# Two mixer layers and a mixture of experts: other DRAM layouts for the reloads, rows fetched earlier from one token tensor, a gate computed in a later stage

## The chip, the cores and the metric

The kernel runs on one core of a Trainium2 chip. Time is the device time of one execution in microseconds (us), the median of several runs. The core has five engines: PE (matrix products; weight loads are listed as PEld), DVE (vector), ACT (activation functions and copies), POOL (general, also issues the indirect transfers) and SP (issues most of the plain transfers). They run in parallel, each in its own program order, and wait for each other by semaphores. Transfers between DRAM and on-chip memory run on 16 DMA engines.

## The reference, cut to what matters

The input is four images of 256 channels and 64 x 64 positions, so 16384 tokens. Everything is float32.

```python
# layer 0: a selective-scan mixer of 512 channels and 16 states, gated by z
tokens = x.transpose(0, 2, 3, 1).reshape(Bb, Hh * Ww, Cc) @ w_in.T
z = sigmoid(silu(tokens @ w_gate.T + b_gate))
t = layernorm(tokens) * ln_g + ln_b
xm, zm = split(t @ in_w.T)
xm = silu(causal_conv4(xm))                    # four taps
dt = softplus(dbl[..., :16] @ dt_w.T + dt_b)   # dbl = xm @ xproj_w.T; B and C are its rest
h = exp(dt * A) * h + (dt * xm) * B            # along the tokens, per channel and state
y = (sum_over_states(h * C) + D * xm) * silu(zm)
x = x + tokens + (y @ out_w.T) * z @ w_out.T
# layer 1: a second mixer with 8 heads and 64 states, then a mixture of 8 experts
t = t + mixer1(layernorm(t))
e = argmax(softmax(layernorm(t) @ gate_w + gate_b))     # one expert per token, with a capacity
t = t + nan_to_num(prob * (relu(layernorm(t) @ w1[e] + b1[e]) @ w2[e] + b2[e]))
```

## The kernel before, in words

The kernel has three phases one after the other: `mixers` (both mixers and the routing), `experts` and `turn` (the result is transposed back into the image layout).

In `mixers` the tokens are cut into 64 chunks of T = 256 tokens, channels on the 128 partitions. A chunk passes through `front0` (input product, layer norm, the first convolution), `mid0` (dt and u), `scan`, `tail0`, `front1`, `ssd` and `back1`. The order of instructions on each engine is not the order of the code: all operations are noted in a `Plan`, each with a time slot (`k_.at(n)`, 16 slots to a chunk, n relative to the chunk's first scan step), an estimated duration and its dependencies, and a list scheduler (`Plan.order`) puts them in an order in which several chunks overlap. This is why nearly all instructions of the mixers carry line 373. FRONT0, MID0, TAIL, SSD and BACK are the first slots of the stages; loads are noted AHEAD = 4 slots early. A tile has a tag and a number of buffers; a new tile of a tag waits until an old one is free.

Data that must move to other partitions goes through DRAM. The convolution wants four taps of 32 channels on 128 partitions: `to_taps` (685) stores `raw`, and `tapped` (691) loads `raw4`, four channel groups with four DMAs, one for each tap. The scan works on tiles of 32 channels x 4 states on the partitions and 4 channel groups x 256 tokens along them: `mid0` stores dt, u and the B and C rows, and `scan` (832) loads `dt4`, `u4` and `bc4`, four DMAs each, and `gx` (silu(zm) and xm). One scan step `u` of 16 is: ACT makes four decays `da`, DVE multiplies `ub` and runs the scan `h`, POOL multiplies `p` by C, PE sums over the states into `py`. There are two buffers each of dt4, u4, gx and h, three of da and p. In `ssd` the decays of layer 1 are summed, stored as `sums_d` and loaded as `cdec`, once for each half chunk.

In all these DRAM tensors the 256 tokens of one channel are contiguous, so that a partition is filled in runs of 1 KB.

The gate `z` of layer 0 is multiplied in `front0` (733) into the first two rows of `pre0`, goes through silu and, by `half_tanh`, to tanh, is stored as `z_d` and reloaded in `tail0`, where x is loaded once more (`xtail`). `silus` (649) gathers the silu calls, since they need a table load on ACT before and behind them; no other table function may stand between.

`back1` stores a chunk's tokens twice, as `tok_d` (the tokens) and `out_d` (where the experts' results go), and POOL scatters for each token a small record `meta` (probability, scale, shift, token number) into the slots of its expert.

`experts` runs over 72 blocks, 63 of 256 slots and 9 of 128, in the order of `line_up`. This phase is ordered by the tile framework's own scheduler. `ahead` (1378) gathers a block's `meta`, casts the token number to an integer (`number`, four buffers) and gathers the expert's weights `w`, 2.2 MB; `begin` (1390) gathers the tokens `rows` from `tok_d`, normalizes them on ACT (`tn`), and has PE transpose them (`pt`, `xt`). Then PE makes the eight hidden products `ph` (ReLU on ACT and DVE: `hid`), and the output product `po`; DVE and ACT make `y` and `fixed`, adding `rows`, and POOL scatters the result to `out_d`. Gathers and scatters are indirect DMAs on POOL's queue, two per block of 256.

`turn` loads 1024 tokens at a time from `out_d`, transposes them on PE and stores the image.

Of the kernel before, what the change touches and what calls it, by code (L numbers as in the profile page):

```python
# [43 lines left out]
TAIL, SSD, BACK = 18, 29, 37  # L44
# [332 lines left out]
def tile_conv_attn_hybrid(ctx: ExitStack, tc: tile.TileContext, a: dict, out: bass.AP, cap: int, st: int):  # L377
# [6 lines left out]
    NB, _, L = x.shape  # L384
    NCH = L // T
# [13 lines left out]
    out_d = dram1.tile([NT, C], F32, name="out_d")  # L399
# [25 lines left out]
    def mixers(es):  # L425
# [215 lines left out]
        def load_x(k_, tag):  # L641
            xin = work([P, KC, T], tag)
            r.dma("SP", xin, x[k_.b].rearrange("(k p) l -> p k l", p=P)[:, :, k_.c * T : (k_.c + 1) * T])
            return xin
# [4 lines left out]
        def silus(*tiles, gates=0):  # L649

            def weight(t):
                return 0.06 + Plan.width(t) / 1130

            load = 1.3
            calls = [(weight(t), nc.scalar.activation, (t, t, AF.Silu), t, t) for t in tiles]
            calls += [(weight(t[:, :KC]), half_tanh, (t[:, :KC],), t[:, :KC], t[:, :KC]) for t in tiles[:gates]]
            calls[0] = (calls[0][0] + load, *calls[0][1:])
            calls.append((load, nc.scalar.preload_act_table_set, (SETS,), None, None))
            r.acts(calls)
# [21 lines left out]
        def spread_rows(d):  # L681

            return d.rearrange("(j g) c l -> (g c) j l", g=SQ)

        def to_taps(raw, tag):

            d = scratch([raw.shape[1] * SQ, R, TAPS - 1 + T], tag)
            r.dma("SP", spread_rows(d), raw)
            return d

        def tapped(d, j):
            t = work([P, SQ, T], "raw4", 3)
            for k in range(TAPS):
                r.dma(
                    "SP",
                    t[k * R : (k + 1) * R],
                    d[j * SQ : (j + 1) * SQ, :, k : k + T].rearrange("g c l -> c g l"),
                )
            return t

        def convolve_taps(raw4, weights, j, dst, bias, get):
            pi = get(T)
            for i in range(SQ):
                r.mm(pi[i * R : (i + 1) * R], weights[:, j * SQ + i], raw4[:, i], start=True, stop=True)
# [15 lines left out]
        def front0(k_):  # L720
# [11 lines left out]
            k_.pre0 = pre0 = work([P, KC + 2 * KD, T], "pre0")  # L732
            pg = bank_a(KC, T)
            for m in range(KC):
                for k in range(KC):
                    r.mm(pg[:, m], w_gate[:, k, m * P : (m + 1) * P], xin[:, k], start=k == 0, stop=k == KC - 1)
            for m in range(KC):
                r.act(pre0[:, m], pg[:, m], AF.Identity, bias=b_gate[:, m : m + 1])
# [10 lines left out]
            for half in range(2):  # L749
                k_.at(FRONT0 + 3 + half)  # L750
                for mp in range(2):
# [6 lines left out]
                    for m in range(2):  # L758
                        j = mp * 2 + m
                        o = half * KD + j  # L760
                        dst = raw[:, j, TAPS - 1 :] if half == 0 else pre0[:, KC + j]
# [4 lines left out]
            for j in range(KD):  # L766
# [3 lines left out]
                convolve_taps(part, taps_m, j, pre0[:, KC + KD + j], m_cb, bank_a)  # L770

        def mid0(k_):

            pre0 = k_.pre0
            xs = pre0[:, KC + KD :]

            k_.at(MID0)
            k_.gx_d = scratch([2 * KD, P, T], "gx_d")
            r.dma("SP", k_.gx_d.rearrange("k p l -> p k l"), pre0[:, KC:])
            k_.z_d = scratch([KC, P, T], "z_d")  # L780
            r.dma("SP", k_.z_d.rearrange("k p l -> p k l"), pre0[:, :KC])
# [3 lines left out]
            for k in range(KD):  # L785
                r.mm(pd[:rows], m_xp[:, k], xs[:, k], start=k == 0, stop=k == KD - 1)
# [3 lines left out]
            r.dma("SP", k_.bc_d.rearrange("p s q l -> (p s q) l"), dbl[DTK:])  # L790
            e = work([P, KD, T], "mid", 2)
            dt = work([P, KD, T], "mid", 2)
            for mp in range(2):
# [18 lines left out]
                r.gps("tensor_tensor", e[:, two], dt[:, two], xs[:, two], ALU.mult)  # L812
            k_.at(MID0 + 6)
            k_.dt_d = scratch([NG, R, T], "dt_d")
            r.dma("SP", spread_rows(k_.dt_d), dt)
            k_.at(MID0 + 7)
            k_.u_d = scratch([NG, R, T], "u_d")
            r.dma("SP", spread_rows(k_.u_d), e)
# [13 lines left out]
        def scan(k_):  # L832
# [3 lines left out]
            for fp in range(2):  # L836
                k_.at(fp * 4 - AHEAD)
                t = work([P, SQ, T], "bc4", 3)
                for q in range(SQ):
                    src = k_.bc_d[fp, :, q]  # L840
# [3 lines left out]
            for jp in range(2):  # L844
                loaded = []
                for jj in range(2):
                    j = jp * 2 + jj
                    both = []
                    for name, src in (("dt4", k_.dt_d), ("u4", k_.u_d)):
                        k_.at(jp * 8 + jj * 2 - AHEAD)  # L850
                        t = work([P, SQ, T], name, 2)
                        for q in range(SQ):
                            r.dma(
                                "SP", t[q * R : (q + 1) * R], src[j * SQ : (j + 1) * SQ].rearrange("g c l -> c g l")
                            )
# [3 lines left out]
                gx = work([P, 2, 2, T], "gx", 2)  # L859
                for s in range(2):  # L860
                    r.dma("SP", gx[:, s], k_.gx_d[s * KD + jp * 2 : s * KD + jp * 2 + 2].rearrange("j p l -> p j l"))
# [11 lines left out]
                for i in range(8):  # L873
# [25 lines left out]
                    if i == 0:  # L899
                        py = bank_y(2, T)  # L900
                        for n in range(2):
                            r.act(py[:, n], gx[:, 1, n], AF.Copy, scale=m_d[:, jp * 2 + n : jp * 2 + n + 1])
# [10 lines left out]
                r.tt(k_.g[:, jp * 2 : jp * 2 + 2], gx[:, 0], py, ALU.mult)  # L913

        def tail0(k_):

            k_.at(TAIL - AHEAD)
            xin = load_x(k_, "xtail")
            z = work([P, KC, T], "z")
            r.dma("SP", z, k_.z_d.rearrange("k p l -> p k l"))  # L920
# [117 lines left out]
        def ssd(k_):  # L1038
# [21 lines left out]
            r.dma("SP", sums_d, sums[:NH])  # L1060
# [8 lines left out]
            for s in range(NS):  # L1069
# [15 lines left out]
                cdec = work([P, hh, Q], "cdec")  # L1085
                for g, hs in enumerate(halves):
                    r.dma("SP", cdec[hs], sums_d[g::2, sl].partition_broadcast(N2))
# [7 lines left out]
                r.gps("tensor_tensor", cdec, cdec, cc[:, None, sl].to_broadcast([P, hh, Q]), ALU.mult)  # L1095
# [22 lines left out]
                for h in range(NH):  # L1118
                    hs, q = halves[h % 2], h // 2
                    r.mm(half(h), state[hs, q], cdec[hs, q], start=False, stop=h == NH - 1, skip_group_check=True)  # L1120
# [14 lines left out]
        def back1(k_):  # L1135
# [23 lines left out]
            for dst in (tok_d, out_d):  # L1159
                r.dma("SP", dst[i0 * P : i0 * P + T].rearrange("(s p) d -> p s d", p=P), row[:, :, :C])  # L1160
# [99 lines left out]
        for i in range(len(chunks) + lag):  # L1260
# [4 lines left out]
            todo = []  # L1265
            if one:
                one.at(MID0)
                todo.append(one.pre0)
            if two:
                two.at(SSD - 1)  # L1270
                todo.append(two.pre1)
            if one:
                one.at(MID0)
                silus(one.pre0, gates=1)
            if two:
                two.at(SSD - 1)
                silus(two.pre1)
            if one:
                for stage in (mid0, scan, tail0, front1):
                    stage(one)  # L1280
# [76 lines left out]
    def experts(es):  # L1357
# [20 lines left out]
        def ahead(nj, i):  # L1378

            w = wp.tile([P, W1 + W2 + KF + C], F32, name=nm("w"), tag="w")  # L1380
            row_at, w_at = tables[nj == 1]
            meta = wk.tile([P, 2, META], F32, name=nm("meta"), tag="meta", bufs=4)[:, :nj]
            for j in range(nj):
                gather(meta[:, j], meta_d, row_at[:, i, j : j + 1], NSLOT + P)
            number = wk.tile([P, 2], U32, name=nm("number"), tag="number", bufs=4)[:, :nj]
            nc.vector.tensor_copy(number, meta[:, :, 3])  # L1386
            gather(w, a["w_exp"], w_at[:, i : i + 1], NE * P)
            return nj, w, meta, number

        def begin(nj, w, meta, number):  # L1390

            st = nj * P
            rows = wk.tile([P, 2, C], F32, name=nm("rows"), tag="rows", bufs=4)[:, :nj]
            for j in range(nj):
                gather(rows[:, j], tok_d, number[:, j : j + 1], NT)
            tn = wk.tile([P, 2, C], F32, name=nm("tn"), tag="tn")
# [15 lines left out]
        now = begin(*ahead(*line_up[0][1:]))  # L1412
        soon = ahead(*line_up[1][1:])
        for at, (_, nj, _) in enumerate(line_up):
# [7 lines left out]
            for f in range(KF):  # L1422
                if f == KF // 2 and at + 1 < len(line_up):

                    now = begin(*soon)
                    soon = ahead(*line_up[at + 2][1:]) if at + 2 < len(line_up) else None
# [158 lines left out]
```

## Time and profile before

| | |
|---|---|
| runs | 6423.47, 6443.36, 6457.77 us, median 6443.36 |
| profiled execution | 6421.74 us, its span 6420.0 us |
| mean granted TensorE clock | 0.935 |
| mixers | first token store at 273.0, last at 5181.3 us |
| experts | first gather of rows at 5206.0, last scatter at 6333.0 us |
| output phase | first load at 6335.4 us |
| scan `h` on DVE | 1024 x 2285 ns |
| `ub` on DVE | 1024 x 1224 ns |
| `da` on ACT | 4096 x 499 ns |
| `p` on POOL | 1024 x 2363 ns |
| DMA | 1211721 packets, 1300.87 MB |

A stage's row gives each engine's busy time in a stretch of the span and the number of its instructions. A row of a waits view reads: engine, what waited, `<-` what released it, then total us, number of times and the longest. A row of a timeline reads: start, duration, engine, line, operation, tile written `<-` tiles read, and in brackets how long the engine had been idle before it and what ended that. "SPq" is SP's DMA queue.

### The profile page before, as it was taken

The page shows a single profiled execution, that of the slowest core. Times are in us where ns is not written, and L with a number is a line of the kernel's source. Part 1 is how long each engine was busy: PE and PEld are TensorE (multiplying, and loading weights), DVE is VectorE, ACT ScalarE, POOL GpSimd, SP SyncE. Part 2 cuts the span into 40 slices and gives each one's busy share as a digit, 9 for nine tenths or more (in the row PEclk, how much of TensorE's full clock was granted, in tenths as well). Part 3 has the DMA queues.
Part 4 walks back from the last instruction along what each step waited for, and adds up shares of the span by engine and source line. Part 5 has one row for each costly group of instructions (what it writes and reads, how often), then busy time and mean ns, then how long its engine had stood idle before and what let it go on. Part 6 is the DMA issues. An engine that isn't in the chain of part 4 may idle for free. (4 is left out here: it accounts for less than half of the span.)

```text
span 6420.0 us, 112284 instructions
## 1 busy us (share of the span) xinstructions
PE 5613.1 (87%) x36878; PEld 3886.2 (61%) x36878; DVE 4893.5 (76%) x5926; ACT 4796.8 (75%) x11218; POOL 4441.4 (69%) x4946
## 2 busy tenths in 40 slices
PE   6889888899888899988888888889988869989896
PEld 4555555555555555555555555555655557777775
DVE  5888889888889898888898888898988733333333
ACT  5888889889889898888898888888989622222223
POOL 4778787878777777777777777778778644444441
PEclk7999999999999999999999999999999889999998
DMA  7888888888888888888788788888888545454446
GB/s 183 208 208 210 209 210 225 211 213 210 212 205 224 207 220 209 221 206 216 202 219 213 200 211 212 209 204 216 218 209 214 127 140 181 170 179 175 169 174 257
DMA packets 1211721, 1300.87 MB, mean 203 GB/s; under 512 B 118319, under 2 KB 1186737, under 8 KB 1199746
## 3 DMA queue, kind: packets, MB, share of 16 engines
q1 hardware_dynamic: 1175042, 1082.31, 67.1%
q0 software_dynamic: 31744, 194.60, 8.5%
q10 hardware_dynamic: 4352, 16.78, 0.6%
q8 instruction: 295, 4.83, 0.3%
q14 instruction: 288, 2.36, 0.1%
HBM read 988.33 MB, written 298.62 MB: 200 GB/s over the span
## 5 line engine op out<-in xcount | busy, mean ns | idle before, releaser
L373 DVE TENSOR_TENSOR_SCAN h<-da,ub 128x1024 f32<-128x1024 f32 x1024 | 2340.3, 2285 | 240.4 <-ACT da L373 81.5
L373 POOL TENSOR_TENSOR p<-h,bc 128x1024 f32<-128x1024 f32 x1024 | 2419.4, 2363 | 14.8 <-PE py L373 13.8
L373 ACT ACTIVATE da<-dt,w_m_Alog 128x255 f32<-128x255 f32 x4096 | 1818.9, 499 | 187.0 <-DVE h L373 157.5
L373 DVE TENSOR_TENSOR ub<-u,bb 128x1024 f32<-128x1024 f32 x1024 | 1253.7, 1224 | 92.7 <-DMA u<-u_d 36.9
L373 PE MATMUL py<-p,sum 128*32 128x256 f32 x8192 | 653.5, 403 | 216.6 <-POOL p L373 185.3
L373 POOL COPY hlast<-h 128x4 f32<-128x4 f32 x1024 | 197.0, 192 | 700.3 <-DVE h L373 632.5
L373 PE MATMUL b<-t,w_W_in 128*128 128x256 f32 x2304 | 585.6, 396 | 11.3 <-DVE res L373 2.9
L1429 PE MATMUL ph<-xt,w 128*128 128x256 f32 (+1 forms) x2304 | 519.5, 380 | 83.7 <-ACT hid L1431 83.7
L373 PE MATMUL a<-t,w_m_in_w 128*128 128x256 f32 x2048 | 507.0, 399 | 27.6 <-DVE t L373 17.2
L1398 ACT ACTIVATE tn<-rows,meta 128x256 f32<-128x256 f32 x135 | 80.1, 596 | 599.2 <-DMA rows<-tok_d,number 596.3
L1429 PEld LDWEIGHTS ph<-xt,w 128*128 128x128 f32 x2304 | 428.4, 197 | 152.0 <-ACT hid L1431 96.6
L373 PEld LDWEIGHTS b<-t,w_W_in 128*128 128x128 f32 x2304 | 429.8, 194 | 137.2 <-issue 40.1
L373 PEld LDWEIGHTS py<-p,sum 128*32 128x32 f32 x8192 | 209.6, 111 | 498.2 <-POOL p L373 271.4
L1440 PE MATMUL po<-w,hid 128*128 128x256 f32 x2160 | 482.9, 382 | 0.0
L373 PEld LDWEIGHTS a<-t,w_m_in_w 128*128 128x128 f32 x2048 | 388.5, 196 | 143.6 <-DVE t L373 37.9
L1440 PEld LDWEIGHTS po<-w,hid 128*128 128x128 f32 x2160 | 413.5, 192 | 56.8
L1452 POOL DMA_INDIRECT out_d<-fixed,number x135 | 138.6, 1027 | 446.4 <-DVE fixed L1450 345.1
L373 ACT ACTIVATE cum<-upto,da 128x128 f32<-128x128 f32 x1024 | 334.9, 391 | 3.2 <-POOL da L373 2.7
L373 ACT ACT_TABLE_LOAD x256 | 328.4, 1283 | 3.9
L373 POOL TENSOR_TENSOR decay<-decay,gm 128x1024 f32<-128x1024 f32 x128 | 302.5, 2363 | 21.3 <-DVE gm L373 16.5
L1386 DVE CAST number<-meta 128x2 uint32<-128x2 f32 x72 | 12.0, 167 | 396.1 <-DMA out_d<-fixed,number 390.1
L1431 ACT ACTIVATE hid<-ph,w 128x256 f32<-128x256 f32 (+1 forms) x432 | 187.0, 453 | 169.7 <-PE ph L1429 169.4
(246 smaller groups left out, 10954.7 us busy)
## 6 DMA issues: line engine op xcount, KB each, us to landing
raw<-raw_d SPq DMA_DIRECT2D x2304, 128.0 KB
dt<-dt_d SPq DMA_DIRECT2D x1024, 128.0 KB
u<-u_d SPq DMA_DIRECT2D x1024, 128.0 KB
gx_d<-pre SPq DMA_DIRECT2D x64, 1024.0 KB
bc<-bc_d SPq DMA_DIRECT2D x512, 128.0 KB
gx<-gx_d SPq DMA_DIRECT2D x256, 256.0 KB
raw_d<-raw SPq DMA_DIRECT2D x64, 647.5 KB
raw_d<-raw SPq DMA_DIRECT2D x64, 518.0 KB
```

The source lines that it names most:

```text
L373: f(*map(placed, args), **{k: placed(v) for k, v in kw.items()})
L1386: nc.vector.tensor_copy(number, meta[:, :, 3])
L1398: act(tn[:, j], rows[:, j], AF.Identity, scale=meta[:, j, 1:2], bias=meta[:, j, 2:3])
L1429: mm(ph, w1[:, k, f * P : (f + 1) * P], xt[:, k], start=k == 0, stop=k == KC - 1)
L1431: act(hid[:, f], ph, AF.Relu, bias=b1[:, f : f + 1])
L1440: mm(po[:, j], hid[:, f, j * P : (j + 1) * P], w2[:, f], start=f == 0, stop=f == KF - 1)
L1452: nc.gpsimd.indirect_dma_start(out=out_d, out_offset=bass.IndirectOffsetOnAxis(ap=number[:, j : j + 1], axis=0), in_=fixed[:, j], in_offse ...
```

## The change

- The DRAM tensors of the reloads get another order of axes, so that what one partition of a tile needs is contiguous: 4 KB for `raw4` (1033 floats, which takes in the padding between groups), `dt4`, `u4`, `bc4`, `gx` and `cdec`. The stores of raw, dt and u become four DMAs of 32 partitions each (`spread`); `gx_d` is stored in 8 KB runs; x is laid out on the host so that a chunk is loaded in 2 KB runs. `cdec` is loaded once per chunk for both halves.
- The gate is multiplied in a new stage `gates`, from slot 10, out of `xtail` and into its own tile `z`; its silu and tanh join the call of the older chunk's `pre1`. `z_d` goes. TAIL is 17. `tail0` and `front1` are noted one chunk later (`mate`).
- In `experts`, `ahead` is split: `find` gathers meta and casts number, `fetch` gathers rows and weights; blocks are found three and fetched two ahead. number and meta have six buffers.
- `out_d` goes: results are scattered into `tok_d`, and `turn` reads that.

```diff
-TAIL, SSD, BACK = 18, 29, 37
+GATE, TAIL, SSD, BACK = 10, 17, 29, 37
...
+        def spread(d, src):
+            for g in range(SQ):
+                r.dma("SP", d[:, :, g], src[g * R : (g + 1) * R])
+        W4 = SQ * (TAPS - 1 + T)
...
-            d = scratch([raw.shape[1] * SQ, R, TAPS - 1 + T], tag)
-            r.dma("SP", spread_rows(d), raw)
+            d = scratch([R, raw.shape[1], SQ, TAPS - 1 + T], tag)
+            spread(d, raw)
...
-            t = work([P, SQ, T], "raw4", 3)
+            t = work([P, W4], "raw4", 3)
+            src = d[:, j].rearrange("c g l -> c (g l)", like=[R, W4])
             for k in range(TAPS):
-                r.dma("SP", t[k * R : (k + 1) * R],
-                    d[j * SQ : (j + 1) * SQ, :, k : k + T].rearrange("g c l -> c g l"))
+                r.dma("SP", t[k * R : (k + 1) * R, : W4 - TAPS + 1], src[:, k : k + W4 - TAPS + 1])
...
-            k_.gx_d = scratch([2 * KD, P, T], "gx_d")
-            r.dma("SP", k_.gx_d.rearrange("k p l -> p k l"), pre0[:, KC:])
-            k_.z_d = scratch([KC, P, T], "z_d")
-            r.dma("SP", k_.z_d.rearrange("k p l -> p k l"), pre0[:, :KC])
+            k_.gx_d = scratch([P, 2 * KD, T], "gx_d")
+            r.dma("SP", k_.gx_d, pre0)
...
-            k_.dt_d = scratch([NG, R, T], "dt_d")
-            r.dma("SP", spread_rows(k_.dt_d), dt)
+            k_.dt_d = scratch([R, KD, SQ, T], "dt_d")
+            spread(k_.dt_d, dt)
...
-                            r.dma("SP", t[q * R : (q + 1) * R], src[j * SQ : (j + 1) * SQ].rearrange("g c l -> c g l"))
+                            r.dma("SP", t[q * R : (q + 1) * R], src[:, j])
...
+        def gates(k_):
+            k_.at(GATE - AHEAD)
+            k_.xtail = load_x(k_, "xtail")
+            k_.at(GATE)
+            k_.z = z = work([P, KC, T], "z")
+            pg = bank_b(KC, T)
+            for m in range(KC):
+                for k in range(KC):
+                    r.mm(pg[:, m], w_gate[:, k, m * P : (m + 1) * P], k_.xtail[:, k], start=k == 0, stop=k == KC - 1)
+            for m in range(KC):
+                r.act(z[:, m], pg[:, m], AF.Identity, bias=b_gate[:, m : m + 1])
...
-            for dst in (tok_d, out_d):
-                r.dma("SP", dst[i0 * P : i0 * P + T].rearrange("(s p) d -> p s d", p=P), row[:, :, :C])
+            r.dma("SP", tok_d[i0 * P : i0 * P + T].rearrange("(s p) d -> p s d", p=P), row[:, :, :C])
...
+            mate = chunks[i - 1] if 0 < i <= len(chunks) else None
             if one:
                 one.at(MID0)
-                silus(one.pre0, gates=1)
-            if two:
-                two.at(SSD - 1)
-                silus(two.pre1)
+                silus(one.pre0)
+            if mate:
+                gates(mate)
+            if two or mate:
+                (two or mate).at(SSD - 1 if two else GATE + 1)
+                silus(*([two.pre1] if two else []), *([mate.z] if mate else []), halves=[mate.z] if mate else [])
...
+        def find(nj, i):
...
+            number = wk.tile([P, 2], U32, name=nm("number"), tag="number", bufs=6)[:, :nj]
+            nc.vector.tensor_copy(number, meta[:, :, 3])
+            return nj, w_at[:, i : i + 1], meta, number
+        def fetch(nj, w_at, meta, number):
+            w = wp.tile([P, W1 + W2 + KF + C], F32, name=nm("w"), tag="w")
+            rows = wk.tile([P, 2, C], F32, name=nm("rows"), tag="rows", bufs=4)[:, :nj]
+            for j in range(nj):
+                gather(rows[:, j], tok_d, number[:, j : j + 1], NT)
+            gather(w, a["w_exp"], w_at, NE * P)
+            return nj, w, rows, meta, number
...
-                    now = begin(*soon)
-                    soon = ahead(*line_up[at + 2][1:]) if at + 2 < len(line_up) else None
+                    now = begin(*got[1])
+                    got = [got[1], fetch(*found[2]) if found[2] else None]
+                    found = [*found[1:], find(*line_up[at + 3][1:]) if at + 3 < len(line_up) else None]
...
-                    out=out_d,
+                    out=tok_d,
```

## Prediction

> **What bounds the kernel now.** I read the slices of the span first, then the table of stages, then who waited for whom in the middle of the mixers, then the experts in order of time. The profiled execution took 6421.74 us, its span 6420.0; the median of the three runs, 6443.36, lies 21.6 us above it. I sum against the profiled execution and carry the 21.6 us to the forecast.
>
> The table of stages (length, then busy us and count of PE, PEld, DVE, ACT, POOL, then the granted clock, the DMA share and GB/s):
>
> ```profile
> 2000.00:3000.00 1000.00, 895.49 (x6367) 585.60 (x6365) 887.57 (x997) 888.33 (x2093) 783.17 (x874) 0.95 0.86 214
> ...
> 5800.00:6000.00 200.00, 180.43 (x839) 156.01 (x838) 70.37 (x142) 55.08 (x127) 83.82 (x83) 0.97 0.48 171
> ```
>
> In the mixers PE, DVE and ACT are each busy 89% at once and the 16 DMA engines 86%: no engine is full, so the stage is bound by three nearly full queues handing work to each other. Stores of a row to the token tensor run from 273.0 to 5181.3 us for 64 chunks: (5181.3 - 273.0) / 63 = **77.9 us per chunk**, of which DVE works 69. In the experts (5200 to 6335) only PE is near full. The output stage takes the last 85 us and keeps its code.
>
> The queues (packets, MB, time as a share of 16 engines' span), then the waits between 1000 and 5000 us (total us, times, longest), DVE, POOL, ACT and PE:
>
> ```profile
> q1 hardware_dynamic: 1175042, 1082.31, 67.1%
> ...
> q10 hardware_dynamic: 4352, 16.78, 0.6%
> ```
>
> ```profile
> DVE h L373 <- POOL p L373: 58.6, 38, 4.2
> ...
> DVE ub L373 <- DMA u<-u_d: 17.9, 11, 4.0
> ```
>
> ```profile
> POOL e L373 <- DMA dt<-dt_d: 39.9, 28, 2.7
> ...
> POOL cdec L373 <- DMA cdec<-sums_d: 13.2, 11, 4.3
> ```
>
> ```profile
> PE a L373 <- DMA raw<-raw_d: 33.3, 18, 3.7
> ```
>
> The reader is to see two things: the DMA engines are busy with small packets, but few engines wait for a DMA, and never long. Experts, in order of time (start, us, engine, line):
>
> ```profile
> 5704.63 1.03 POOL L1452 DMA_INDIRECT out_d<-fixed,number  x1 [5.47 <-DVE fixed L1450]
> ...
> 5708.59 1.03 POOL L1452 DMA_INDIRECT out_d<-fixed,number  x1 [0.30 <-issue]
> ...
> 5711.18 0.17 DVE L1386 CAST number<-meta 128x2 uint32<-128x2 f32 x1 [6.44 <-DMA out_d<-fixed,number]
> ...
> 5711.62 1.02 POOL L1367 DMA_INDIRECT rows<-tok_d,number  x1 [2.01 <-DVE number L1386]
> ...
> 5714.57 0.60 ACT L1398 ACTIVATE tn<-rows,meta 128x256 f32<-128x256 f32 x1 [10.97 <-DMA rows<-tok_d,number]
> 5715.08 0.89 ACT L1443 ACTIVATE y<-y,meta 128x256 f32<-128x256 f32 x2
> ...
> 5720.77 1.03 POOL L1452 DMA_INDIRECT out_d<-fixed,number  x1 [5.52 <-DVE fixed L1450]
> ```
>
> This is a loop, and it sets the pace: y to first scatter 5.69, first to second scatter 3.96, second scatter through its landing and the cast of number (whose buffer that scatter still reads) to the gather of rows 3.03, rows landing 2.95, normalizing before the next y 0.51. Sum 16.14 us, and scatter to scatter is 5720.77 - 5704.63 = 16.14. PE's own work for such a block, from the last blocks (po starts 6303.44 and 6317.26, no transposes between), is 13.8, about 14.4 with them.
>
> **The change in the mixers.** Packets first. 67.1% x 16 x 6420 us / 1175042 = 58.7 ns for a packet of 0.92 KB; queue 10 moves 4 KB packets, 0.6% (0.55 to 0.65) x 16 x 6420 / 4352 = 130 to 153 ns. Per chunk the reloads of raw (36 DMAs of 128 KB), dt, u (16 each) and bc (8) fall from 128 packets each to 32, gx from 1024 packets to 256, cdec from 1024 to 128, gx_d from 1024 of 1 KB to 128 of 8 KB. Adding the untouched ones, about 16600 data packets become about 5800: some 2800 of 4 KB x 0.142 = 400, 128 of 8 KB x 0.28 = 36, 2560 of 1 KB x 0.062 = 159, 256 of 2 KB x 0.09 = 23 (8 and 2 KB are estimates from the two measured sizes), in all about 620 engine-us of 16 x 77 = 1230. The DMA share should go from 0.86 to about **0.5** (0.45 to 0.62).
>
> What that is worth is where a rule and the rows part. The Trainium skill (Perfetto Trace Analysis, DMA Optimizations) says transfers under 2 KB carry significant overhead and that going to 4 KB can "dramatically improve throughput" when DMA-bound. Were the mixers DMA-bound, a chunk would fall to DVE's 69 us: 64 x 8.9 = -570 us. The rows say otherwise. In 4000 us (51.4 chunks) DVE waited for DMAs 23 us (u 17.9, dt 3.0, raw 2.3), POOL 70 (dt 39.9, cc 16.4, cdec 13.2), ACT 24 (dt 16.6, bc 7.7), PE 49 (raw 40.1, cc 8.5). cc is not touched; the rest is 0.45 us per chunk on DVE and 2.3 on the others. I count DVE's whole and half of the others', because POOL is a fifth idle and its lateness reaches DVE only through rows like h <- p: 0.45 + 1.15 = 1.6 us x 64 = **-102 us**, bounds -29 (DVE's own alone) and -176 (all of it). What is late next is ACT's da and PE's results, which are computed, not fetched.
>
> Added and moved. Stores of raw, dt and u become four DMAs of 32 partitions: 12 more issues of 0.36 to 0.43 us on SP per chunk; removed are z_d, z, the second token store, two gx and two cdec, with one more for sums_d: 99 issues become 105, +2.6 us of SP per chunk. I cost this at 0: SP waits about half of its time for buffers (DVE ub 241 us, ACT da 148 in those 4000). Its bad end: loads of raw, dt and u now wait on SP until four landings, 3 x 0.43 = 1.3 us later for each of four sets, and all other loads stand behind them; 5.2 us x 64 = +333 if nothing covers it. The gate's 8 matmuls and 2 evictions (2.0 + 0.9 us) move from the tiles tagged a (three deep) to b (one deep) and, by chunk, a stage later; the same work, covered by PE's 10% idle time and by b being free about half of a chunk; uncovered 2.9 x 64 = +186, or a gain of some us where a was short (ACT waited 83 us for PE a before pre). I take 0. The silu of z leaves the 2560-wide call and becomes one of its own after pre1: from 2304 in 2.12 and 2560 in 2.34 us the fixed part is 2.12 - 9 x 0.22 = 0.14 us, x 64 = **+9 us**; the four table loads of 1.28 us stay. DVE, POOL and PE get no new operation; gx, cdec and raw4 are only read at other strides: 0. x in 2 KB runs and one fewer token store only empty the DMA engines further, and the output stage reads as many bytes as before: 0. TAIL 17 for 18 and the mates reorder instructions; no row prices that: I allow 40 us either way.
>
> **The change in the experts.** The intent needs rows to be there early. But tokens and results now share one tensor, so each gather of rows must wait for the scatter before it on POOL's queue. The Trainium skill (DMA: Bandwidth & Descriptors, Rules for kernel authors) speaks against it: a DMA that reads what an earlier one wrote must wait for that one's semaphore; the queue does not order them. Where the fetch were free, the sum would gain all of PE's idle time there, 1080 - 979 = 100 us between 5240 and 6320. By the order of the built program: scatter of block 6, both halves, then rows of 9; ACT has tn of 9 ahead of y of 7. So it is still one loop per block: y, scatters, landing, rows, tn, y. Behind the waiting gather stand POOL's second gather, the weights and the next scatter; behind the waiting tn stand y and the ReLUs PE needs. The cast leaves the loop: 5711.62 - 5711.18 = -0.44, so 15.70 us. But in three more blocks of eight both halves of tn now stand ahead of y, so the second gather (1.33 later) counts: 17.03. Per eight blocks: 3 x -0.44 + 3 x +0.89 = +1.3, and about +2 at the single block, where another gather waits for a landing with the weights' transfer ahead of it. +3.4 x 9 = **+30 us**, bounds -32 (each block -0.44) and +64 (each +0.89).
>
> Sum: -102 + 9 + 30 = -63: 6421.7 - 63 = 6359 against the profiled execution, **6380 us** against the median.
>
> **Rivals.**
> - *The loop opens.* If rows do come early, experts -100 and mixers -93: 6250. For it: number has six buffers and the weights move ahead of rows. Against: the order above. Chance 0.18.
> - *SP's fourfold stores (slower).* Place: the first reload of raw, dt or u after its stores. Price 5.2 us per chunk; the forecast's gain is gone from 1.0 us per chunk on DVE, 0.5% slower from 1.5; with half of it through (+166): 6546. For it: SP waited 69 us for landings of raw_d already. Against: its slack. Chance 0.18.
> - *The transfers were hidden anyway.* Only DVE's own waits go (-29), experts +30, ACT +9: 6453. Speaks for it: the widest DVE waits are for ACT and POOL. Chance 0.12.
>
> **How the numbers follow.** The forecast has 0.52, its own range 6300 to 6450. The range 6240 to 6490 leaves out about half of the first rival's mass and most of the second's. A measurement tells 0.5% (32 us) from no change. Faster: 0.17 from the first rival and 0.39 of the forecast, 0.56; same: 0.10 of the forecast, 0.10 of the third, 0.20; slower: the rest, 0.24.
>
> **What would show it.** Right: chunk period near 76.4, DMA share 0.45 to 0.62 in the mixers, POOL e <- DMA dt near nothing; in the experts a scatter-to-scatter step between 15.7 and 17.1, rows waiting for the token tensor's scatter instead of number. Wrong: DMA share low with an unchanged chunk (third rival), SP waiting longer on raw_d (second), PE over 95% busy in the experts (first).

## The result, and the profile after

The changed kernel takes 6654.02 us (median of four runs, 6643.98 to 6664.2) against 6446.19 us: ratio **1.0327, 95% interval 1.0294 to 1.036**, slower. The forecast was 6380 us, its range 6240 to 6490. The profiled execution has a span of 6662.2 us (6420.0 before).

The stages, from the trace as in the prediction: token stores run from 264.0 to 5372.7 us, (5372.7 - 264.0) / 63 = 81.1 us per chunk (77.9 before), so the mixers end 191 us later. From the first gather of rows to the last scatter of the experts it is 1177 us (1127 before). The output phase still takes 85 us.

First the table of stages of the changed kernel (stretch, its length, then busy us and number of instructions of PE, PEld, DVE, ACT, POOL, granted clock, DMA share, GB/s):

```profile
2000.00:3000.00 1000.00, 862.42 (x6021) 549.59 (x6019) 841.24 (x952) 850.70 (x2003) 745.82 (x832) 0.94 0.76 194
6000.00:6200.00 200.00, 176.68 (x808) 148.33 (x809) 67.15 (x133) 53.71 (x120) 82.76 (x82) 0.97 0.46 164
```

and the queue that carries the mixers' transfers (packets, MB, time as a share of 16 engines' span), from its page:

```profile
q1 hardware_dynamic: 483842, 1034.65, 60.6%
```

DVE did 952 operations in that millisecond instead of 997; every engine works 4 to 6% less. No engine took the others' place: they all wait more. In the experts PE works 177 of 200 us, where it worked 180 in the stretch shown before. The packets of this queue fell to 41% of before, roughly as the forecast counted, but their time fell from 67.1% to 60.6% only: 0.606 x 16 x 6662.2 / 483842 = 133.5 ns for a mean packet of 2.14 KB, where it was 58.7 ns for 0.92 KB.

The waits between 1000 and 5000 us (total us, times, longest), first two rows of the kernel before, then the changed kernel:

```profile
DVE h L373 <- ACT da L373: 65.2, 52, 4.7
...
POOL cdec L373 <- DMA cc<-pre: 16.4, 8, 3.7
```

```profile
DVE h L373 <- ACT da L373: 131.1, 71, 5.1
POOL cdec L373 <- DMA cc<-pre: 126.4, 37, 6.9
...
DVE ub L373 <- DMA u<-u_d: 66.1, 30, 6.2
...
PE a L373 <- DMA raw<-raw_d: 61.7, 24, 5.1
...
DVE g L373 <- PE py L373: 52.9, 28, 4.1
...
POOL e L373 <- DMA dt<-dt_d: 33.1, 28, 3.3
...
DVE h L373 <- POOL p L373: 27.3, 28, 2.8
```

The waits for transfers, which the change was to shorten, grew: u from 17.9 to 66.1 us and raw on PE from 33.3 to 61.7. Only dt (39.9 before) is a little shorter. POOL's wait for cc, a transfer that the change does not touch, grew from 16.4 to 126.4, and h waits twice as long for ACT's da. Faster or not, these transfers come later.

The experts of the changed kernel on POOL, in order of time (start, us, engine, line, operation, and in brackets the idle time before it and what ended it):

```profile
5706.46 1.02 POOL L1453 DMA_INDIRECT tok_d<-fixed,number  x1 [6.36 <-DVE fixed L1451]
...
5710.41 1.02 POOL L1453 DMA_INDIRECT tok_d<-fixed,number  x1 [0.30 <-issue]
5713.14 1.02 POOL L1362 DMA_INDIRECT rows<-tok_d,number  x1 [1.70 <-DMA tok_d<-fixed,number]
```

The gather of rows, though of a block fetched two ahead, stands behind the scatter and is released by its landing. That is the place at which the loop of the forecast closes.

### The profile page after: what moved, and what is told of

It is laid out like the page before. It is cut to its first block, busy times and chain, and to the rows that moved or that the text cites. A ratio compares the mean times of both kernels' runs of the same rounds, so it can differ in the third digit from the quotient of the medians.

```text
span 6662.2 us, 112787 instructions
## 1 busy us (share of the span) xinstructions
PE 5691.9 (85%) x36878; PEld 3852.4 (58%) x36878; DVE 4878.4 (73%) x5926; ACT 4835.8 (73%) x11284; POOL 4440.4 (67%) x4946
## 3 DMA queue, kind: packets, MB, share of 16 engines
q1 hardware_dynamic: 483842, 1034.65, 60.6%
## 4 chain that ended last, share of the span: by engine, by line
PE 25%; DMA 18%; DVE 17%; ACT 13%; issue 13%; POOL 7%; SPq 6%; POOLq 0%; DVEq 0%; ACTq 0%
PE a L373 13%; DVE h L373 9%; PE b L373 8%; SPq L373 6%; DMA raw<-raw_d 5%; DVE ub L373 5%; ACT da L373 3%; DMA rows<-tok_d,number 2%; ACT pre L373 2%; POOL p L373 2%; DMA u<-u_d 2%; DMA dt<-dt_d 2%; DMA tok_d<-fixed,number 2%; PE po L1441 1%; PE py L373 1%
## 5 line engine op out<-in xcount | busy, mean ns | idle before, releaser
L1453 POOL DMA_INDIRECT tok_d<-fixed,number x135 | 137.8, 1020 | 442.5 <-DVE fixed L1451 343.9
L373 PE MATMUL a<-cum,after 128*128 128x512 f32 x512 | 308.3, 702 | 35.1 <-DVE state L373 31.1
L373 PE MATMUL b<-g,w_m_out_w 128*128 128x256 f32 x1024 | 303.6, 459 | 8.3 <-DVE g L373 8.3
```

The source lines that it names most:

```text
L373: f(*map(placed, args), **{k: placed(v) for k, v in kw.items()})
L1453: nc.gpsimd.indirect_dma_start(out=tok_d, out_offset=bass.IndirectOffsetOnAxis(ap=number[:, j : j + 1], axis=0), in_=fixed[:, j], in_offse ...
```

## The experiments

All ratios are to the kernel before, run on the same chip; us are (ratio - 1) x 6440. "Chunk" is (last - first token store) / 63 in each run's one profiled execution; 77.9 before, whose profiled execution lies 25 us under its median.

| run | ratio | 95% interval | us | chunk, us | clock |
|---|---|---|---|---|---|
| changed kernel | 1.0327 | 1.0294-1.036 | +211 | 81.1 | 0.928 |
| layouts_alone | 1.0262 | 1.0236-1.0288 | +169 | 80.6 | 0.925 |
| gate_alone | 0.9943 | 0.9922-0.9964 | -37 | 77.4 | 0.949 |
| experts_one | 1.0052 | 1.0034-1.007 | +33 | 77.7 | 0.935 |
| experts_two | 0.995 | 0.9933-0.9967 | -32 | 78.0 | 0.937 |
| split_stores | 1.0443 | 1.0417-1.0469 | +285 | 81.8 | 0.913 |
| long_loads | 0.9971 | 0.9957-0.9985 | -19 | 78.0 | 0.939 |
| layouts_a5 | 0.987 | 0.985-0.989 | -84 | 76.5 | 0.946 |
| gate_two | 0.9881 | 0.986-0.9902 | -77 | 77.8 | 0.948 |
| split_unplanned | 1.0125 | 1.0102-1.0147 | +80 | 79.3 | 0.931 |
| after_cdec_old | 1.0242 | 1.0218-1.0266 | +156 | 79.7 | 0.937 |
| layouts_a5_two | 0.9821 | 0.9798-0.9843 | -115 | 76.2 | 0.947 |
| after_unplanned_a5_two | 1.0069 | 1.0046-1.0091 | +44 | 79.3 | 0.940 |
| layouts_unplanned | 1.0186 | 1.0166-1.0207 | +120 | 80.1 | 0.929 |
| before_a5 | 1.0159 | 1.0141-1.0177 | +102 | 79.4 | 0.933 |
| gate_two_a6 | 0.9737 | 0.9721-0.9754 | -169 | 76.2 | 0.949 |
| split_unplanned_raw | 1.005 | 1.0036-1.0064 | +32 | 78.7 | 0.933 |
| split_unplanned_dtu | 1.0078 | 1.0064-1.0091 | +50 | 78.9 | 0.935 |
| split_free | 1.0171 | 1.0155-1.0187 | +110 | 80.2 | 0.928 |

### Which part loses it

Four kernels, each the kernel before with one part of the change: the layouts (cdec left as it was), the gate, the experts, and the experts with the second token tensor kept:

```diff
 experts_two, against experts_one
+    out_d = dram1.tile([NT, C], F32, name="out_d")
...
-                    out=tok_d,
+                    out=out_d,
```

> The kernel before with the new layouts alone: raw, dt, u, B and C, gx, z and x in long runs, dt, u and raw stored by four DMAs each; the gate, cdec, both token stores and the experts as before. The change lost 191 us in the mixers. If the layouts lose it (theory L: the long runs are hardly cheaper for a DMA engine, 16.0 against 15.7 GB/s, and each load lands later or is issued later), this one is slower by 130 to 200 us, ratio about 1.02 to 1.03, and DVE and POOL wait more for DMAs. If the gate's move loses it (theory G), this one is faster by 30 to 100 us, ratio 0.985 to 0.995, which is what the prediction said of the layouts.

> The kernel before with the gate's move alone: multiplied from slot 10 into a tile tagged b, silu and tanh in one call with the older chunk's pre1, TAIL 17, tail0 and front1 noted a chunk later; DRAM layouts, cdec and experts as before. Theory G (b is one deep, cc waits for the longer call, the planner's order is worse): slower by 130 to 200 us, ratio 1.02 to 1.03, with ACT waiting for PE a and POOL cdec for cc about as in the changed kernel (126 us in 1000 to 5000 us against 16). Theory L: within 40 us of before.

> The kernel before with the experts' change alone: found three and fetched two blocks ahead, results scattered into the token tensor, one token store per chunk. The experts took 50 us more in the changed kernel. If that is their own: 40 to 60 us slower, ratio 1.006 to 1.009. If it came from elsewhere (other stores, placement): within 15 us of before.

> The kernel before with rows found three and fetched two blocks ahead, but results still scattered to their own tensor, so that a gather of rows waits for no scatter. If the wait for the scatter on one tensor costs the 50 us (theory R), the loop opens: PE's idle 100 us in the experts go at least in half, 50 to 100 us faster than before, ratio 0.985 to 0.992, and DVE number or POOL rows no longer wait for a scatter. If the order on POOL and ACT costs them (theory O: the second tn and the next block's gathers stand ahead of y and of the scatters), it stays slower by 20 to 50 us, ratio 1.003 to 1.008.

The layouts lose 169 us by themselves; the gate's move gains 37, against theory G. The experts' change loses 33 us (their stage 1171 us for 1127), and with two tensors gains 32 (1091 us). experts_two also stores each chunk's tokens twice again, as the kernel before does. The waits of the experts between 5300 and 6300 us, one tensor, then two:

```profile
ACT tn L1400 <- DMA rows<-tok_d,number: 565.5, 97, 11.5
...
POOL rows L1365 <- DMA tok_d<-fixed,number: 114.9, 62, 4.2
PEld pt L1405 <- ACT tn L1400: 107.9, 88, 3.4
PE pt L1405 <- ACT tn L1400: 79.6, 77, 3.0
```

```profile
DVE number L1385 <- DMA out_d<-fixed,number: 415.5, 48, 9.5
ACT tn L1402 <- DMA rows<-tok_d,number: 348.3, 79, 7.4
...
POOL rows L1367 <- issue: 34.5, 113, 0.3
```

With two tensors no gather of rows waits for a scatter, tn waits 217 us less, and PE's waits for tn are no longer in the list. So the read after write on the one tensor costs 80 us of the stage and 66 of the whole, and theory R holds in its direction. Against the kernel before, the stage gains 36 us instead of the 50 to 100 expected. The cast of number still waits 415.5 us for scatters, so that part of the expected sign did not come; whether it is what holds back the rest was not tested.

### The long runs or the four stores

split_stores cuts only the stores; long_loads lengthens only the loads. It takes 4 KB runs out of tensors that are stored as before, so the channels it loads are mixed up.

```diff
 split_stores, against before
-            r.dma("SP", spread_rows(d), raw)
+            for g in range(SQ):
+                r.dma("SP", d.rearrange("(j g) c l -> g c j l", g=SQ)[g], raw[g * R : (g + 1) * R])
 long_loads, against layouts_alone
-            spread(d, raw)
+            r.dma("SP", spread_rows(d), raw)
...
-            src = d[:, j].rearrange("c g l -> c (g l)", like=[R, W4])
+            src = runs(d)[:, j]    # "(c j g) l -> c j (g l)" of the same rows
```

> The kernel before, with only the stores of raw, dt and u cut into four DMAs of 32 partitions each; all tensors and loads keep their runs of 1 KB, so the DMA engines move the same packets. 12 more DMAs per chunk (112 for 100). Theory S (the four stores lose the time: more to issue on SP, eight outstanding at most, the loads behind them planned and started later): slower by at least the 171 us of the layouts alone less what the long runs may bring, 130 to 300 us, ratio 1.02 to 1.045. Theory P (the long runs lose it): within 30 us of before.

> The kernel with the new layouts alone, but raw, dt and u stored as before, one DMA each; their loads still take 4 KB runs, of the same tensors read as if another order of channels lay in them, so that channels are mixed up and the numbers of the output are others. 98 DMAs per chunk. Theory S: the loss is gone, and what the long runs bring by themselves shows: between 60 us faster and 20 us slower than before, ratio 0.99 to 1.003. Theory P: still slower by 100 us or more, ratio over 1.015.

Theory S. The kernel with long runs and single stores gains 19 us (10 to 28). This is not the long runs alone: the traces of before and long_loads show the operations of DVE, ACT, POOL and SP in different orders, and a kernel with long runs in the order of before was not run. Queue 1 and the stage's row of long_loads:

```profile
q1 hardware_dynamic: 566786, 1084.95, 62.5%
```

```profile
2000.00:3000.00 1000.00, 890.24 (x6279) 582.69 (x6279) 884.33 (x992) 880.06 (x2080) 776.78 (x866) 0.95 0.80 213
```

Half the packets, 0.80 of the DMA engines for 0.86, and the same pace: 992 operations of DVE in the millisecond. The trace's packet records say why, and how little the engines gained (mean and fastest twentieth of queue 1, ns; GB/s from the mean):

| packet | before | long_loads |
|---|---|---|
| 1024 B | 65.2 (46), 15.7 GB/s | 51.2 (46) |
| 4096 B | - | 247.0 (159), 16.6 GB/s |
| 4132 B | - | 265.6 (160), 15.6 GB/s |

At their fastest, 4 KB in 159 ns is 16% more per ns than 1 KB in 46. On the average the gain is none to 6%: the long packets took 1.55 to 1.66 times their best time, the short ones of before 1.42 times. From the same records a reload of dt lands 3.73 us after its issue (median; 3.87 before), u 3.51 (3.73), raw 3.98 (4.14), so the flight itself, from issue to landing, became only 0.14 to 0.22 us shorter. Nor did the waits become shorter: between 1000 and 5000 us DVE, POOL, ACT and PE waited 194 us for transfers before and 208 in long_loads. These sums, unlike the 19 us, say directly that there was little to gain.

What four separate stores can do to the order is seen on SP, in order of time, in split_stores (only the lines of dt; between them stand loads of other chunks):

```profile
2150.09 0.32 SPq L373 DMA_DIRECT2D dt_d<-mid  x1
...
2154.25 0.72 SPq L373 DMA_DIRECT2D dt_d<-mid  x1
...
2157.54 0.43 SPq L373 DMA_DIRECT2D dt_d<-mid  x1
...
2161.40 0.43 SPq L373 DMA_DIRECT2D dt_d<-mid  x1
...
2171.19 1.87 SPq L373 DMA_DIRECT2D dt<-dt_d  x4
```

The plan has put them 11 us apart. So split_stores holds two things: issues, and an order. The next kernels part these.

### Issues or order

In split_unplanned the four DMAs are one operation for the plan, so the order on every engine is that of the kernel before; two more kernels do this for raw alone and for dt and u alone. layouts_unplanned does it in the new layouts. split_free names each part of a store to the plan as its own piece of the tensor; in split_stores each part had named all of it, so that the plan set each behind the landing of the one before, an order that the changed kernel doesn't have.

```diff
 split_unplanned, against before
-            r.dma("SP", spread_rows(d), raw)
+            def four(d, src):
+                d = d.rearrange("(j g) c l -> g c j l", g=SQ)
+                for g in range(SQ):
+                    nc.sync.dma_start(d[g], src[g * R : (g + 1) * R])
+            r.note("SP", 0.47, four, (d, raw), {}, (d,), (raw,), lag=...)
```

> The kernel before with the stores of raw, dt and u cut into four DMAs each, as in split_stores, but the four of a store noted to the plan as one operation of one store's weight and landing time: the order of all other instructions on every engine is that of the kernel before, and only three more issues stand behind each store on SP. Theory order (the four notes shift the plan's order of loads and tiles, and that loses the time): within 65 us of before, ratio 0.99 to 1.01. Theory issue (12 more issues and landings per chunk on SP and its eight lanes lose it whatever the order): most of the 282 us of split_stores remain, ratio 1.025 to 1.045. My own guess by now: in between, nearer to order, about 1.01.

> As split_unplanned (the order of the kernel before kept), but only the two stores of raw are cut in four; 6 more issues per chunk. If the price of the four issues is the lateness of raw's reload, which the plan puts close behind its store: most of the 80 us, 50 to 90 us slower, ratio 1.008 to 1.014. If it is SP's time or its lanes, whichever store it is: half, 30 to 50 us, 1.004 to 1.008.

> As split_unplanned, but only the stores of dt and u are cut in four; 6 more issues per chunk. If the lateness of raw's reload is the price: within 25 us of before, ratio 0.998 to 1.004, because dt and u have 9 us and more between landing and reload. If it is SP's time or its lanes: 30 to 50 us, 1.004 to 1.008.

> The kernel before with the stores of raw, dt and u cut into four DMAs each, 1 KB runs, each part named to the plan as its own piece of the tensor (as in the changed kernel), so that none waits for another. If the four stores are the layouts' whole loss: 1.0262 / 0.9971 = 1.029, slower by 160 to 210 us. If the order made around four independent notes costs as little as between layouts_unplanned and layouts_alone (49 us): 80 + 49 = about 130 us, ratio 1.017 to 1.023. If most of split_stores' loss was the chained notes: about the 80 us of split_unplanned, 1.010 to 1.016.

> The new layouts alone, with the four stores of raw, dt and u noted to the plan as one operation; AHEAD 4. The order of the kernel long_loads, and 12 more issues per chunk. If the parts add up, 0.9971 x 1.0125 = 1.0095: 60 us slower than before (40 to 80), so that of the 171 us some 110 are the order made around four notes, 80 the issuing, and -19 the long runs. If four stores and long runs together cost something of their own: 1.02 to 1.03 remain.

The traces bear out the kept order: in the mixers DVE, ACT, POOL and SP run the same sequence of operations in before and split_unplanned, and in long_loads and layouts_unplanned, but for the added stores. The order kept, the 12 issues cost 80 us (66 to 95): 1.25 us per chunk. They add up, 32 for raw's six and 50 for the six of dt and u, so it is not raw's close reload that pays, as one theory had it, but something that every store costs: SP's time, or its places for transfers in flight (the traces never show more than eight of SP's at once). The record speaks for the time. Between 1000 and 5000 us SP's waits for landings of transfers fell from 277 to 230 us, while its issues took 633 of each 1000 us instead of 578. With the plan free to arrange them, 110 us. The rest of split_stores' 285 was its own chained order.

In the long layouts the same 12 issues cost more: layouts_unplanned against long_loads, same order, 1.0186 - 0.9971 or 138 us, and the order made around four notes another 1.0262 - 1.0186 or 49 us. So the layouts' 169 us are -19 + 138 + 49, within 1 us. The sum expected of layouts_unplanned (1.0095) failed, by 59 us. A part of this the traces show: a quarter of a store into the new layout takes SP longer to issue. Stores of raw on SP in before, split_unplanned and layouts_unplanned (start, us, queue, line, operation, number of DMAs):

```profile
3010.61 0.38 SPq L373 DMA_DIRECT2D raw_d<-raw  x1
```

```profile
2189.15 1.94 SPq L690 DMA_DIRECT2D raw_d<-raw  x4
```

```profile
2152.68 2.63 SPq L686 DMA_DIRECT2D raw_d<-raw  x4
```

The median issue of a quarter took 0.44 us in split_unplanned and 0.60 in layouts_unplanned (0.60 in the changed kernel too), so that the stores of raw, dt and u take 7.7 and 10.0 us of SP per chunk, where single stores take 1.7. If the price goes by these added 5.9 and 8.3 us, 80 us become about 112, an estimate; the remaining 26 of the 138 are hardly outside the intervals. No run tests it.

The waits between 1000 and 5000 us where it shows, in split_unplanned, then in split_free:

```profile
POOL e L373 <- DMA dt<-dt_d: 59.3, 34, 4.3
...
PE a L373 <- DMA raw<-raw_d: 50.0, 25, 5.2
...
PE b L373 <- DMA raw<-raw_d: 44.4, 26, 3.4
...
DVE ub L373 <- DMA u<-u_d: 42.9, 19, 5.9
```

```profile
POOL e L373 <- DMA dt<-dt_d: 110.2, 48, 6.4
...
DVE ub L373 <- DMA u<-u_d: 73.1, 23, 13.4
```

With the order kept, u is waited for 42.9 us instead of 17.9 and dt 59.3 instead of 39.9; with the new order both more. These are transfers of 1 KB packets, as before, and in split_unplanned they fly no longer: a reload of dt lands 3.68 us after its issue (median; 3.87 before), u 3.48 (3.73). What is late is their issue.

### The order by itself

AHEAD is the number of slots by which loads are noted before their use. Changing it moves no work and adds none.

```diff
-AHEAD = 4
+AHEAD = 5
```

> The kernel with the new layouts alone, with AHEAD 5 instead of 4: the same DMAs, the loads of the scan and of the tail noted a slot (a sixteenth of a chunk, 5 us) earlier. If the loss comes from loads that are issued too late behind the four stores (theory S, in its form of order): at least half of the 171 us comes back, ratio to before 0.99 to 1.013. If it comes from the work of issuing or moving itself, an earlier slot changes nothing: 1.02 to 1.03.

> The kernel before with AHEAD 5 and nothing else. If the gain of layouts_a5 belonged to AHEAD 5 itself: 50 to 100 us faster than before, ratio 0.985 to 0.992. If an order is good or bad for one set of operations only, and the slot has to fit the stores: not faster, 0 to 110 us slower, ratio 1.0 to 1.017.

The same number that gains 252 us in the layouts (1.0262 to 0.987) loses 102 in the kernel before. It is not a better value for both; the order must fit the operations. In layouts_a5 the four stores and the long runs are all there, SP's issues take more of each 1000 us rather than less (655 between 1000 and 5000 us, for 630 in layouts_alone), and its row is as full as that of the kernel before:

```profile
2000.00:3000.00 1000.00, 894.31 (x6406) 584.15 (x6404) 892.21 (x1000) 890.90 (x2099) 786.86 (x878) 0.96 0.84 216
```

DVE does 1000 operations (957 in layouts_alone). So the changed layouts don't have to lose, and the price of the four stores is a price in a given order: at AHEAD 4 it is paid, at AHEAD 5 an order was found that more than hides it.

### cdec, and versions that beat both

```diff
 after_cdec_old, against the changed kernel
-            for g in range(2):
-                r.dma("SP", sums_d[g * hh : (g + 1) * hh], sums[g:NH:2])
-            cdec = work([P, hh, T], "cdec")
+            r.dma("SP", sums_d, sums[:NH])
...
+                cdec = work([P, hh, Q], "cdec")     # once for each half
```

> The changed kernel with cdec loaded in two halves from one store of sums_d, as before; all else is the changed kernel's. The parts measured alone give 1.0262 x 0.9943 x 1.0052 = 1.0257 against 1.0327 for all: 45 us are left over. If the one load of cdec with its earlier place causes them (POOL waited 126 us for cc before it multiplies cdec, 16 before): ratio to before 1.022 to 1.029. If it is how the parts meet in the plan: 1.03 to 1.036.

> The changed kernel with three things altered: the four stores of raw, dt and u noted to the plan as one, AHEAD 5, and the experts' results in a tensor of their own. If the changed kernel's loss is the order made around the four stores and the wait for the scatter, all of it goes: faster than before by 60 to 150 us, ratio 0.976 to 0.991. If the four issues themselves cost, it stays above 1.0.

> The gate's move and the fetching two blocks ahead with results in their own tensor, the two parts that gained by themselves (-33 and -27 us), without the layouts and without the one token tensor. If they add up: about 60 us faster than before, ratio 0.988 to 0.992, and faster than both kernels of the case.

> The new layouts with AHEAD 5 and rows fetched two blocks ahead with results in their own tensor; gate and cdec as before. layouts_a5 gained 85 us and experts_two 27 us: if they add up, 112 us faster than before, ratio 0.980 to 0.985, the fastest so far.

> The gate's move and rows fetched two blocks ahead with results in their own tensor, with AHEAD 6; no new layouts (1 KB runs, one store each). gate_two was at 0.9881 with AHEAD 4. If the order alone decides: 30 to 80 us better than that, ratio 0.975 to 0.984, as fast as layouts_a5_two (0.9821) or faster. If the long runs are what made layouts_a5_two fast: 0.985 to 0.992.

Loading cdec once for both halves costs 1.0327 - 1.0242, 55 us, and when it is undone, cdec's wait for cc is gone from the list. Whether it is the one load or its earlier place in the plan was not parted. The parts then give 169 - 37 + 33 + 55 = 220 us, measured 211.

after_unplanned_a5_two was to be faster and is 44 us slower. In it three of four issues are hidden from the plan; in layouts_a5 they are counted, and it is fast. That an order made without them is one that SP can't keep would fit split_unplanned, but is not shown here: the kernel has the new gate and cdec as well, and which of these costs what was not tried.

gate_two adds its two parts (-37 and -32, measured -77). layouts_a5_two is at 6308 us. **gate_two_a6** is the fastest: 6272.38 us, 0.9737, without any of the new layouts:

```profile
2000.00:3000.00 1000.00, 902.29 (x6465) 581.23 (x6466) 899.24 (x1027) 906.68 (x2147) 799.58 (x894) 0.96 0.84 211
```

1027 operations of DVE in the millisecond, with packets of 1 KB. The gate, an experts' loop without the read after write, and a fitting order are worth 169 us. No version with long runs reached this, but none was run at AHEAD 6, and none with the new gate and its four stores counted by the plan at AHEAD 5; so the runs don't show that long runs are worse at their best.

## Why the prediction was wrong

The sign was wrong: -63 us were forecast and +211 measured. The terms as the runs give them are stores and their order 187 (forecast 0), long runs -19 (-102), cdec 55 (0), gate -37 (+9), experts 33 (+30), together 219. Since each of these kernels has an order of its own, every term has some of that in it. By its own steps:

- **What bounds the kernel** was read rightly: three nearly full queues and no full engine. "The DMA engines are busy with small packets, but few engines wait for a DMA, and never long" was the sentence to hold on to.
- **Packets.** The count was right. The price was not: 4 KB was put at 142 ns, from queue 10, which stores the output in a phase of its own; the reloads took 247 to 266 in long_loads. The DMA share went to 0.76, not to 0.5 (0.45 to 0.62). This term was mis-sized.
- **What that is worth**, -102 us with bounds -29 and -176: long_loads brought 19 us, less than either bound. To count "DVE's whole and half of the others'" was the false part: with long runs POOL waited 44.7 us for dt (39.9 before) and PE 51 for raw (40.1). A wait for a transfer is a wait for its issue, its flight of 3.5 to 4 us and its place behind others; the change shortened the flight by 0.2. The page "Perfetto Trace Analysis", section "DMA Optimizations", of the Trainium skill, with its dramatic gain from 4 KB, was rightly set aside as a bound on time. It also speaks of the size of a whole DMA, and the reloads were DMAs of 128 KB before and after; for their runs, the rate hardly rose (15.7 to between 15.6 and 16.6 GB/s for each engine).
- **The four stores**, "I cost this at 0": **this is the step that failed.** In a kept order they cost 80 us in the old layout and 138 in the new one; with the order made around them 110 and 187. These are prices in the orders of AHEAD 4; at AHEAD 5, in layouts_a5, the same stores stand in a kernel that gains 84 us. The cover named, that SP waits about half of its time, was read too high and is an average: between 1000 and 5000 us SP waited 1555 us of 4000, 39%, and issued for 58%. SP is in order: a load behind a store that waits is late however idle SP is elsewhere. An issue was also put at 0.36 to 0.43 us, and took 0.60. The second rival had the right cause, SP's stores, but neither its price nor its sign. Its 5.2 us per chunk were 1.25 to 2.2, and SP did not wait longer for the landing of raw_d (before, then the changed kernel):

```profile
SPq L373 <- DMA raw_d<-raw: 69.2, 63, 3.7
```

```profile
SPq L373 <- DMA raw_d<-raw: 7.8, 12, 1.3
```

That the second rival's 6546 is the nearest of the four sums is luck in part, since the plan's order and cdec, which it does not count, add to the loss.

- **The plan's order**, "no row prices that: I allow 40 us either way": before_a5 is 102 us, layouts_alone to layouts_a5 252. It was mis-sized by a factor of 2.5 to 6, and it was the largest unknown of the case.
- **cdec**, priced as strides and two DMAs fewer, at 0: 55 us.
- **The gate**, 0 and +9: -37. The gain named as possible ("where a was short") fits: ACT's wait of pre for PE a fell (before, then gate_alone). Order is in it too.

```profile
ACT pre L373 <- PE a L373: 83.0, 88, 2.8
```

```profile
ACT pre L373 <- PE a L373: 61.0, 81, 2.7
```

- **The experts**, +30 by one loop per block: 33 in experts_one, and the loop is there, rows behind the landing of the scatter. This step was right, and so was the rule drawn from the Trainium skill (DMA: Bandwidth & Descriptors, Rules for kernel authors), that a DMA reading what an earlier one wrote must wait for that one to land: in experts_one gathers of rows waited 62 times for a scatter, 114.9 us in all. The first rival, the loop opens, needed the second tensor; then it brought 32 us, a third of its 100.
- **The third rival**, the transfers were hidden anyway, is right of the transfers (it allowed 29 us, and 19 came). It lost because the stores, the order and cdec were not free.

## What to carry to other kernels

Before giving transfers longer runs, find what is waited for: the flight or the issue. If it is the issue, a DMA added on an in-order queue can cost a part of its length even where the queue waits 39% of the time (here 80 us for 768 issues of 0.48 us on the mean, 22%, in an order not made for them). And in a kernel whose order is made by a list scheduler, each change of operations is also a draw of a new order; here one slot number was worth up to 252 us, more than any part of the change. Compare after tuning the slots for both, or keep the order fixed.

## What was not expected of the hardware

- In long_loads packets of 4 KB, most of them into 32 partitions, took 247 ns on the mean where the fastest twentieth took 159; packets of 1 KB took 51 there and 65 in before, where the fastest took 46. On the mean, four times the size took 3.8 to 4.8 times as long.
- A store of dt or u of 32 partitions (128 KB) lands 2.6 to 2.9 us after its issue (medians of split_unplanned), one of 128 partitions (512 KB) 3.9 to 4.2 (before). A quarter of the bytes takes 0.62 to 0.76 of the time.
- A store of 32 partitions took SP 0.60 us to issue into the new layout (layouts_unplanned) and 0.44 into the old one (split_unplanned), medians, for the same bytes.
- The mean granted clock followed the pace roughly: 0.913 in the slowest kernel (split_stores), 0.935 before, 0.949 in the fastest (gate_two_a6), but 0.949 in gate_alone too, which is 133 us slower than that one by their ratios, and 0.937 in after_cdec_old, which is slower than before. Which drives which the runs don't tell.
